# A four-layer graph kernel: products of the second pass during the neighbour search, norms on four row groups, and r and c of the last chunk from unscaled rows

## The chip, the cores and the metric

The kernel runs on one core of a Trainium2 chip. The metric is the time of one execution on the device in microseconds (us); lower is better. A core has TensorE (PE, matrix products; its weight loads are shown as PEld), VectorE (DVE), ScalarE (ACT), GpSimd (POOL), SyncE (SP, which here only issues transfers) and sixteen DMA engines. Each engine works through its own queue in order; between engines the program sets semaphores.

## The reference, cut to what matters

x is 2708 x 128, adj 2708 x 2708, both 32-bit floats. Four layers follow one another, each `x = layernorm(x + layer(x, adj))`. The change touches the first and the start of the second.

```python
def _L0_gnn_ref(x, A, W1, b1, W2, b2, sigma, k):       # sigma = 1, k = 4
    z = _lap_mul(A, x) @ W1 + b1                        # _lap_mul: d * (A @ (d * x)), d = 1/sqrt(row sums)
    z = leaky_relu(z, negative_slope=0.1)
    sq = sum(z * z, axis=-1)
    d2 = maximum(sq[:, None] + sq[None, :] - 2.0 * (z @ z.T), 0.0)
    S = exp(-sqrt(d2 + 1e-10) / (2.0 * sigma))
    S = where(ranks of -S in the row < k, S, 0.0)       # the k nearest of each node
    return _lap_mul(S + A, x) @ W2 + b2

def _L1_gnn_ref(X, A, W, a):
    XW = X @ W
    s_col, s_row = XW @ a[0, :f], XW @ a[0, f:]
    den = exp(leaky_relu(s_row[:, None] + s_col[None, :], negative_slope=0.01))
    num = A @ den
    att = where(num != 0, den / num, 0.0)
    return A @ (att @ XW)
```

The third layer is a normalised A times x times a matrix, the fourth a product of x and A @ x with a matrix, then a maximum with zero.

## The kernel before

**Tiles and chunks.** The 2708 nodes are 22 row tiles of 128 (`T`); the last, number 21 (`FULL`), has 20 rows (`LAST`). The columns are six chunks (`C`), four of 512 and one each of 384 (tiles 16 to 18) and 276 (tiles 19 to 21). Rows of the transposed adjacency for tiles 0 to 15 (`S` = 16) are streamed from memory in panels of four tiles by one chunk (`load_panel`, L171, issued by SP); those for tiles 16 to 21 stay in memory on the core (`res`).

**First pass and search (layer 0).** A first pass sums degrees and computes z, its transpose zT, and the negated square norms (`nsq`). `nsq3` holds the norms as three bf16 parts on three partitions; a product with ones (`ones3`) adds them to every row. The search runs over 22 tiles, in the order 4 to 15, 0 to 3, 16 to 21 (L623). For each, TensorE makes six norm products (L632) and six products of zT with itself (L642) into six accumulators, ACT copies these into a `key` tile (L643, three buffers), and VectorE finds the eight largest values of each row (MAX8, L644) and their places (FIND_INDEX8, L645). `z2`, the doubled rows, is made by ACT (L626).

**Weights.** `weigh` (L586) turns the distances of a batch of tiles into similarities (two operations on VectorE, a logarithm and two exponentials on ACT), degrees, and the scaled rows y2, writes these to `y2_rows` in memory, and calls `others` (L556), which separates the node itself from its neighbours. It runs in batches: tiles 0 to 16 after tile 16, 17 to 19 after tile 19, 20 and 21 at the end. A scheduler places the instructions of the search on each engine.

**Second pass.** `by_panels` (L189, products at L204) multiplies the adjacency with y2, chunk by chunk: 21 products a chunk, and one round for the 20 last rows for each group of three chunks (chunks share a call through the row groups, `few`). For chunk 0 the order is tiles 0 to 11, 16 to 19, 12 to 15, 20. Beside it runs a list of due work, `Due`: each product is a tick, and work is entered by its tick. `sum_near` (L678) adds, for each tile, three gathered rows of neighbours (L672, an indirect transfer by POOL, nine buffers) with weights on VectorE; it is due at ticks 24 + 23t/5. `end_pass2` (L825) enters, for each chunk: `finish` (add the neighbour sums with identity products, L692, and copy to `hT`, L832), `norm0` (product with W2, residual, layer norm), `turn` (transposes into `xT`), `find_c` (c, the column scores, on all rows, and its own entry `cc`), `times_w` and `keep_xw` (XW and its rows to memory), and for each tile `compare` (a 0/1 mask of c against the node's own c, L779; ties counted in L781), `rank_rows` (ACT sums the mask's rows, L792) and `rank_columns` (products with ones sum its columns into `rk`, L797). With both sums c of every node gets its rank. For the last tile `compare` sums its rows on VectorE itself (L774). The order on TensorE, VectorE and ACT is that of the program here.

**After the pass.** Ranks are put together (L918 to L923), `pick_c` (L927) picks c at some ranks, first "head", then "first", `to_all` and `on_all` spread values over the partitions by products, `gb` and `lc` are filled, and the sums of layer 1 by blocks of ranks run over the panels again (L1176), with further work put between them (`between`).

Of the kernel before, what the change touches and what calls it, by code (L numbers as in the profile page):

```python
# [8 lines left out]
F32 = mybir.dt.float32  # L9
# [21 lines left out]
class Due:  # L31


    def __init__(self):
        self.n, self.work = 0, []

    def at(self, n, f, *args):
        self.work.append((n, len(self.work), f, args))
        self.work.sort(key=lambda w: w[:2])
# [13 lines left out]
def kernel(  # L53
# [54 lines left out]
    mis_pool = psum.enter_context(tc.tile_pool(name="mis", bufs=2, space=bass.MemoryType.PSUM))  # L108
# [80 lines left out]
    def by_panels(weights, done, tick=None, ready=(), first=None):  # L189
# [6 lines left out]
        accs = {}  # L196

        def product(c, i, src, w):
            lhsT = weights(i)[few(c) if i == FULL else slice(None)]
            start = c not in accs  # L200
            if start:
                accs[c] = acc_tile()
            stop = tick is None and i == (FULL if c % GROUPS == 0 else FULL - 1)
            nc.tensor.matmul(accs[c][: lhsT.shape[-1], :w], lhsT=lhsT, rhs=src, start=start, stop=stop)  # L204

        for c in range(C):
            w = cw[c]
            for i in [*(first if first and c == 0 else range(FULL)), *([FULL] if c % GROUPS == 0 else [])]:
                if i == FULL:
                    for n in range(c, c + GROUPS):  # L210
                        product(n, i, res[few(n), i - S, cols[n]], cw[n])
                    done(c, accs[c])
                    for _ in range(GROUPS if tick is not None else 0):
                        tick()
                    continue
                if i < S:
                    if i % 4 == 0:
                        if ready:
                            part = ready.pop(0)
                        else:  # L220
                            part = load_panel(i // 4, c)
                    src = part[:, i % 4, :w]
                else:
                    src = res[:, i - S, cols[c]]
                product(c, i, src, w)
                if i == FULL - 1 and c % GROUPS:
                    done(c, accs[c])
                if tick is not None:
                    tick()

# [133 lines left out]
    with tc.tile_pool(name="knn", bufs=1) as knn:  # L364
        nsq = knn.tile([P, T], F32, tag="nsq", name="nsq")
        nsq3 = knn.tile([3, N], BF16, tag="nsq3", name="nsq3")
        ones3 = knn.tile([3, P], BF16, tag="ones3", name="ones3")
# [47 lines left out]
        def turn_norms(c, ts, parts):  # L415
# [4 lines left out]
            nc.scalar.copy(nsq3[:, cols[c]], ps[:3, : cw[c]])  # L420
# [1198 lines left out]
```

## Time and profile before

| what | us |
| --- | --- |
| median of seven runs | 1061.82 (1056.93 to 1068.3) |
| the profiled execution, time / span | 1063.85 / 1062.1 |
| PE busy / PEld busy in the span | 990.8 / 479.7 |
| DVE / ACT / POOL busy | 643.0 / 338.8 / 265.5 |
| search: first MAX8 starts, last FIND_INDEX8 ends | 167.61, 301.54 |
| second pass on PE: first product, end of the last identity products | 294.71, 421.70 |
| last copy to hT ends | 422.53 |
| "head" of the ranks starts | 439.27 |
| clock granted to TensorE, mean | 0.974 of full |

Times inside the span count from its start. A row of the groups names the line, the engine, the operation, its output and inputs with shapes, the count, then busy time, mean nanoseconds of one, and the engine's idle time just before such instructions with what ended most of it. A row of the timeline has start, duration, engine, line, operation, shapes and count, and in brackets the idle time ahead of it with its releaser. Products in 32-bit floats are two records each.

In the window 157 to 301.6, the search, PE is busy 143.38 us, DVE 136.41, ACT 78.36 and POOL 15.95 of 144.60.

### The profile page before, as it was taken

To read this page: it belongs to the slowest core of one execution; us is meant where nothing else is said; L and a number is where in the kernel's file an instruction comes from. 1 tells how busy PE (TensorE), PEld (TensorE's weight loads), DVE (VectorE), ACT (ScalarE), POOL (GpSimd) and SP (SyncE) were. 2 spreads that over 40 slices of the span, in tenths; PEclk is the share of its full clock that TensorE was granted. 3 is DMA by queue.
4 is the path that set the end of the run, shared out by engine and by line. 5 is a ranking of instruction groups with operands and counts; after the bars stand their busy time and mean duration, and the time that the engine had idled before them with its cause. 6 is when DMAs were issued, how large, how long until landed. Compare 5 with 4: busy or idle time off the path is not lost.

```text
span 1062.1 us, 11424 instructions
## 1 busy us (share of the span) xinstructions
PE 990.8 (93%) x3678; PEld 479.7 (45%) x3678; DVE 643.0 (61%) x1351; ACT 338.8 (32%) x614; POOL 265.5 (25%) x332
## 2 busy tenths in 40 slices
PE   0888999999999998699899999999999999999996
PEld 0346454444444556344333333334445544564444
DVE  5985438999965577763999999994111121222222
ACT  0000125555511246413767777662010100020000
POOL 4000000000457762117864444430121100000000
PEclk9989999999999999699999999999999999998998
DMA  9999350000068766399465545566565957574662
GB/s 339 365 343 250 113 174 1 0 1 0 11 217 262 224 179 216 136 350 277 129 180 132 143 136 168 137 173 219 197 218 145 316 170 228 144 261 147 225 174 67
DMA packets 109363, 190.30 MB, mean 179 GB/s; under 512 B 13650, under 2 KB 46690, under 8 KB 109294
## 3 DMA queue, kind: packets, MB, share of 16 engines
q1 hardware_dynamic: 91408, 151.79, 44.0%
q0 software_dynamic: 17712, 37.62, 12.8%
q8 instruction: 31, 0.51, 0.2%
q14 instruction: 38, 0.31, 0.1%
q10 hardware_dynamic: 174, 0.08, 0.0%
HBM read 214.37 MB, written 4.16 MB: 206 GB/s over the span
## 4 chain that ended last, share of the span: by engine, by line
PE 83%; DVE 5%; DMA 5%; POOL 3%; issue 2%; ACT 2%; SPq 0%; POOLq 0%; DVEq 0%; ACTq 0%
PE acc L204 36%; PE acc L642 9%; PE hacc L1280 9%; PE num L1423 8%; PE acc L428 8%; PE acc L632 2%; PE acc L1176 2%; DMA res<-in_adjT 2%; DMA ring<-in_adjT,slot_i 1%; PE mis L285 1%; DMA part<-in_adjT 1%; DVE mask L779 1%; DVE both L483 1%; POOL ring L125 1%; PE mis L1187 1%
## 5 line engine op out<-in xcount | busy, mean ns | idle before, releaser
L1301 POOL DMA_INDIRECT ring<-in_adjT,slot_i x88 | 98.3, 1116 | 100.6 <-PE num L1423 84.3
L1423 PE MATMUL num<-ring,lw 128*64 128x512 f32 (+1 forms) x528 | 113.7, 551 | 3.4 <-DVE err L1265 1.8
L1280 PE MATMUL hacc<-inv,xws 128*128 128x512 f32 (+1 forms) x264 | 111.7, 559 | 0.3 <-ACT inv L1258 0.3
L642 PE MATMUL acc<-zT,z 128*128 128x512 f32 (+4 forms) x264 | 108.3, 557 | 0.0
L1255 ACT ACTIVATE inv<-num,plain 128x1024 f32<-128x1024 f32 x88 | 80.5, 915 | 59.2 <-PE num L1423 56.5
L253 POOL TENSOR_TENSOR rstd<-rstd,minus_half 128x4 f32<-128x4 f32 (+1 forms) x19 | 18.2, 956 | 316.6 <-DVE rstd L252 316.6
L234 ACT COPY gb<-acc 128x512 f32<-128x512 f32 (+2 forms) x18 | 9.6, 534 | 252.7 <-PE acc L204 252.7
L643 ACT COPY key<-acc 128x512 f32<-128x512 f32 (+3 forms) x132 | 70.1, 534 | 59.8 <-issue 29.8
L204 PE MATMUL acc<-ring,y 128*128 128x512 f32 (+2 forms) x192 | 81.8, 555 | 0.5 <-POOL sim L579 0.5
L1265 DVE TENSOR_TENSOR err<-inv,num 128x1024 f32<-128x1024 f32 x88 | 74.4, 855 | 13.0 <-ACT inv L1258 12.3
L1280 PEld LDWEIGHTS hacc<-inv,xws 128*128 128x128 f32 x264 | 46.5, 189 | 77.2 <-issue 37.0
L204 PE MATMUL acc<-ring,xs 128*128 128x512 f32 (+2 forms) x192 | 78.2, 551 | 0.0
L1272 DVE SCALAR_TENSOR_TENSOR inv<-gb,g_inv,inv 128x1024 f32<-128x1024 f32 x88 | 77.1, 914 | 0.1
L672 POOL DMA_INDIRECT got<-y_rows,where x66 | 70.2, 1063 | 25.7 <-issue 8.2
L204 PE MATMUL acc<-ring,carry 128*128 128x512 f32 (+2 forms) x192 | 74.5, 542 | 0.0
L204 PE MATMUL acc<-ring,m_rows 128*128 128x512 f32 (+2 forms) x192 | 74.3, 542 | 0.0
L1269 DVE SCALAR_TENSOR_TENSOR inv<-err,inv 128x1024 f32<-128x1024 f32 x88 | 72.7, 865 | 0.1
L642 PEld LDWEIGHTS acc<-zT,z 128*128 128x128 f32 (+1 forms) x264 | 47.5, 188 | 55.0 <-issue 49.5
L570 POOL TENSOR_TENSOR slot_e<-near,sim 128x44 f32<-128x44 f32 (+2 forms) x3 | 0.7, 241 | 271.5 <-DVE d2inv L598 267.4
L1258 ACT ACTIVATE inv<-inv 128x1024 f32<-128x1024 f32 x88 | 67.6, 768 | 2.8
L644 DVE MAX8 near<-key 128x8 f32<-128x2708 f32 (+1 forms) x22 | 65.5, 2979 | 4.8 <-ACT key L643 4.8
L645 DVE FIND_INDEX8 where<-near,key 128x8 uint32<-128x2708 f32 (+1 forms) x22 | 65.4, 2972 | 0.0
(327 smaller groups left out, 1339.3 us busy)
## 6 DMA issues: line engine op xcount, KB each, us to landing
ring<-in_adjT SPq DMA_DIRECT2D x86, 1024.0 KB
ring<-in_adjT SPq DMA_DIRECT2D x19, 768.0 KB
part<-in_adjT SPq DMA_DIRECT2D x12, 1024.0 KB
ring<-in_adjT SPq DMA_DIRECT2D x19, 552.0 KB
res<-in_adjT SPq DMA_DIRECT2D x4, 1280.0 KB
more<-in_adjT SPq DMA_DIRECT2D x4, 1024.0 KB
part<-in_adjT SPq DMA_DIRECT2D x3, 768.0 KB
part<-in_adjT SPq DMA_DIRECT2D x3, 552.0 KB
```

The source lines that it names most:

```text
L204: nc.tensor.matmul(accs[c][: lhsT.shape[-1], :w], lhsT=lhsT, rhs=src, start=start, stop=stop)
L428: nc.tensor.matmul(accs[c][:, : cw[c]], lhsT=y[:, i, :], rhs=src[:, : cw[c]], start=first, stop=last)
L642: nc.tensor.matmul(pks[c][:p, : cw[c]], lhsT=z2[:, :p], rhs=zT[:, cs], start=False, stop=True)
L643: nc.scalar.copy(key[:p, cs], pks[c][:p, : cw[c]])
L672: nc.gpsimd.indirect_dma_start(out=got[:p, :], out_offset=None, in_=y2_rows[:, :], in_offset=bass.IndirectOffsetOnAxis(ap=where[:p, t, k : ...
L1255: nc.scalar.activation(inv, num[:, :w], AF.Ln, scale=plain[:, 0:1], bias=plain[:, 1:2])
L1265: nc.vector.tensor_mul(err, inv, num[:, :w])
L1269: nc.vector.scalar_tensor_tensor(inv, err, 2.0, inv, op0=ALU.subtract, op1=ALU.mult)
L1272: nc.vector.scalar_tensor_tensor(inv, gb[:, col : col + w], g_inv[:, q : q + 1], inv, op0=ALU.max, op1=ALU.mult)
L1280: nc.tensor.matmul(haccs[:, o:e], lhsT=xws[:, q, :], rhs=inv[:, o:e], start=(q == 0), stop=(q == NQ - 1))
L1301: nc.gpsimd.indirect_dma_start(out=rows[i][:KC, n, :], out_offset=None, in_=adj_half[:, :], in_offset=bass.IndirectOffsetOnAxis(ap=slot_i[ ...
L1423: nc.tensor.matmul(num[n * (BJ + 2) : (n + 1) * (BJ + 2), o:e], lhsT=lw[:, 2 * q + n, :], rhs=rows[i][:, n, c0 + o : c0 + e], start=True, ...
```

## The change

- The norm products lie on four row groups: the norm rows and the ones are held at partitions 0, 32, 64 and 96, copied there by three transfers on SP's queue ahead of the panels. Tile 4, the first of the search, still uses the first group alone.
- Twelve products of chunk 0 of the second pass (tiles 4 to 15) are issued during the search, one in each of the tiles 6 to 17 of its order, into an accumulator of their own. The panels of chunk 0 are loaded in the order 1, 2, 3, 0, and a panel of chunk 1 when one is used up. On TensorE the order is that of the program from the second tile.
- `weigh` runs in six calls: tiles 4 to 7, 8 to 11, 12 to 15 and 0 to 3 with their adds on POOL, 16 to 19 and 20 to 21 with their adds on VectorE.
- The second pass takes chunk 0's products of tiles 0 to 3 and 16 to 19, four of chunk 1, then the rest; the due ticks are moved.
- For the last chunk (tiles 19 to 21) the rows are turned before they are normalised; r and c come from products of the raw rows with two columns of weights, corrected with mean and standard deviation. `last_norm` and `last_xw` normalise the rows and make XW later, in the sums of layer 1.
- The mask of tile 20 is made in two halves, the second summed on VectorE. The comparison of tile 21 with all columns is replaced by one of all nodes with its 20 columns (`compare_few`). Rank constants (`fold`, `sel`, `rk_f`) move to the start of the second pass, into the memory of `near`.

The diff, cut to its core:

```diff
-        nsq3 = knn.tile([3, N], BF16, tag="nsq3", name="nsq3")
-        ones3 = knn.tile([3, P], BF16, tag="ones3", name="ones3")
+        NORMS = 4
+        nsq3 = knn.tile([32 * NORMS, N], BF16, tag="nsq3", name="nsq3")
+        ones3 = knn.tile([32 * NORMS, P], BF16, tag="ones3", name="ones3")
...
+        w_rc = wae[:, D:]
+        w_sum = atile([2], "w_sum")
+        ps = mis_tile()
+        nc.tensor.matmul(ps[:, :2], lhsT=ones_f, rhs=w_rc, start=True, stop=True)
+        nc.vector.tensor_copy(w_sum, ps[:, :2])
...
-        def weigh(ts):
+        def weigh(ts, engine):
...
-            nc.vector.tensor_add(nr, nr, nsq[:, t0:t1, None].to_broadcast([P, t1 - t0, TOPK]))
-            nc.vector.tensor_scalar(nr, nr, 0.0, DIST_EPS, op0=ALU.min, op1=ALU.subtract)
+            engine.tensor_add(nr, nr, nsq[:, t0:t1, None].to_broadcast([P, t1 - t0, TOPK]))
+            engine.tensor_scalar(nr, nr, 0.0, DIST_EPS, op0=ALU.min, op1=ALU.subtract)
...
-            nc.vector.tensor_reduce(dd, sm, AX.X, ALU.add)
-            nc.vector.tensor_add(dd, dd, deg[:, t0:t1])
+            if engine is nc.vector:
+                nc.vector.tensor_reduce(dd, sm, AX.X, ALU.add)
+                nc.vector.tensor_add(dd, dd, deg[:, t0:t1])
+            else:
+                engine.tensor_add(dd, sm[:, :, 0], deg[:, t0:t1])
+                for k in range(1, TOPK):
+                    engine.tensor_add(dd, dd, sm[:, :, k])
...
-        ready = [load_panel(g, 0) for g in range(G)]
+        mis_psum.close()
+        first_psum = ExitStack()
+        first_pool = first_psum.enter_context(
+            tc.tile_pool(name="first", bufs=1, space=bass.MemoryType.PSUM, side="right")
+        )
+        acc0 = first_pool.tile([P, CW], F32, tag="first", name="acc0")
+        for g in range(1, NORMS):
+            nc.sync.dma_start(nsq3[32 * g : 32 * g + 3, :], nsq3[:3, :])
+        AHEAD = range(4, S)
+        panels0 = {g: load_panel(g, 0) for g in (*range(1, G), 0)}
+        ready = [panels0[0]]
+        batches = {7: range(4, 8), 11: range(8, 12), 15: range(12, 16), 3: range(4), T - 3: range(S, T - 2)}
...
+                if n == 1:
+                    search.enter_context(tc.manual_schedule(engines={nc.tensor.engine}))
...
-                    cs = cols[c]
-                    nc.tensor.matmul(pks[c][:p, : cw[c]], lhsT=ones3[:, :p], rhs=nsq3[:, cs], start=True, stop=False)
+                    r = slice(32 * (c % NORMS), 32 * (c % NORMS) + 3) if n else slice(3)
+                    nc.tensor.matmul(
+                        pks[c][:p, : cw[c]], lhsT=ones3[r, :p], rhs=nsq3[r, cols[c]], start=True, stop=False
+                    )
...
+                i = n - 2
+                if i in AHEAD:
+                    nc.tensor.matmul(
+                        acc0[:, : cw[0]], lhsT=y2[:, i, :], rhs=panels0[i // 4][:, i % 4, : cw[0]],
+                        start=(i == AHEAD[0]), stop=False,
+                    )
+                    if i % 4 == 3:
+                        ready.append(load_panel(len(ready) - 1, 1))
...
-                if t == T - 6:
-                    weigh(range(0, T - 5))
-                if t == T - 3:
-                    weigh(range(T - 5, T - 2))
-            weigh(range(T - 2, T))
+                if t in batches:
+                    weigh(batches[t], nc.gpsimd if t < T - 3 else nc.vector)
+            weigh(range(T - 2, T), nc.vector)
...
+    spare = near.rearrange("p t k -> p (t k)")
+    few_n, rk_f, neg_r = (spare[:, n * T : (n + 1) * T] for n in range(3))
+    fold, sel = spare[:, 3 * T : 3 * T + 2 * NCH], spare[:, 3 * T + 2 * NCH : 3 * T + 2 * NCH + 2 * NB]
+    nc.vector.memset(rk_f, float(OOB))
+    nc.vector.tensor_add(fold, ident[:, : 2 * NCH], ident[:, 32 : 32 + 2 * NCH])
...
-    def norm0(ts, power=False):
+    def norm0(ts, raw=False):
...
-        normalize(ts, xs, power)
+        if not raw:
+            normalize(ts, xs)
...
+    def rc_of(c, p_of):
+        ts = chunk_tiles[c]
+        po = mis_tile()
+        for k, t in enumerate(ts):
+            p, o = p_of(t), t * P - starts[c]
+            nc.tensor.matmul(po[:p, 2 * k : 2 * k + 2], lhsT=xTs[c][:, o : o + p], rhs=w_rc, start=True, stop=True)
+        return po[:, : 2 * len(ts)].rearrange("p (k v) -> p v k", v=2)
...
+    def last_rc():
+
+        both = rc_of(C - 1, lambda t: P)
+        for v, dst in ((1, cc), (0, rr)):
+            nc.vector.scalar_tensor_tensor(
+                dst[:, l0:l1], mv[:, l0:l1, 0], w_sum[:, v : v + 1], both[:, v, :], op0=ALU.mult, op1=ALU.subtract
+            )
+            nc.vector.scalar_tensor_tensor(
+                dst[:, l0:l1], dst[:, l0:l1], -1.0, rstd_l, op0=ALU.mult, op1=ALU.mult
+            )
+
+    def last_norm():
+        for t in last_ts:
+            nc.vector.tensor_scalar(
+                xs[: pw[t], t, :], xs[: pw[t], t, :], mv[: pw[t], t, 0:1], rstd_l[: pw[t], t - l0 : t - l0 + 1],
+                op0=ALU.subtract, op1=ALU.mult,
+            )
+
+    def turn_c(c):
+
+        pc = mis_tile()
+        for t in chunk_tiles[c]:
             o = t * P - starts[c]
...
+            nc.tensor.transpose(pc[:, o : o + P], cc[:, t : t + 1].to_broadcast([P, P]), ident)
+        nc.scalar.copy(c_row[:, cols[c]], pc[:, : cw[c]])
...
+    split = {T - 2: (T - 1) * P // 2}
...
+        m = split.get(t, o + p)
+        nc.vector.tensor_scalar(mask[:p, :m], c_row[:p, :m], s, None, op0=ALU.is_ge)
+        if m < o + p:
             nc.vector.tensor_scalar(
...
+                mask[:p, m : o + p], c_row[:p, m : o + p], s, 0.0, op0=ALU.is_ge, op1=ALU.add, accum_out=rows_h[:p],
+            )
...
+    def compare_few():
+
+        grid = [P, T, LAST]
...
+        nc.vector.tensor_tensor(
+            few_m, cc[:, :, None].to_broadcast(grid), c_row[:, None, FULL * P :].to_broadcast(grid), op=ALU.is_ge
+        )
+        for u in range(T):
+            nc.tensor.matmul(
+                rk[:LAST, T - 1 : T], lhsT=few_m[: pw[u], u, :], rhs=ones_b[: pw[u], :1], start=False,
+                stop=(u == T - 1), skip_group_check=True,
+            )
+        nc.vector.tensor_reduce(few_n, few_m, AX.X, ALU.add)
+        own_ties(T - 1)
...
-    near_at = [24 + (23 * t) // 5 for t in range(T)]
+    near_at = [23 + (21 * t) // 5 for t in range(T)]
...
-                    at(n + 17 + 2 * k, rank_columns, t)
+                    at(n + (20 if c < C - 2 else 18) + 2 * k, rank_columns, t)
...
-            at(n + 1, exp_table)
             at(n + 2, norm0, ts, True)
-            at(n + 3, turn, c)
-            at(n + 4, find_c, c)
-            for t in ts:
-                at(n + 4, times_w, c, t)
-            at(n + 4, keep_xw, c)
...
+            at(n + 2, turn, c, True)
+            at(n + 2, exp_table)
+            at(n + 2, find_r)
+            at(n + 3, last_stats)
+            at(n + 3, last_rc)
+            at(n + 3, turn_c, c)
+            at(n + 3, negate_r)
+            for k, t in enumerate(ts[:-1]):
+                at(n + 4 + k, compare, t)
+                at(n + 4 + k, rank_rows, t)
+                at(n + 5 + k, rank_columns, t)
+            at(n + 3 + len(ts), compare_few)
+            at(n + 4 + len(ts), exp_r)
...
-        by_panels(
-            rows_of(y2), end_pass2, due.tick, ready, [*range(S - 4), *range(S, T - 2), *range(S - 4, S), T - 2]
-        )
+        tail = [FULL - 1, FULL]
+        order = [*((0, i) for i in (*range(4), *range(S, FULL - 1))), *((1, i) for i in range(4))]
+        order += [*((0, i) for i in tail), *((1, i) for i in range(4, FULL))]
+        order += [(c, i) for c in range(2, C) for i in [*range(FULL), *([FULL] if c % GROUPS == 0 else [])]]
+        by_panels(rows_of(y2), end_pass2, due.tick, ready, order, {0: acc0})
...
         c_part = pick_c(edge, "first")
+        last_norm()
+
+        def last_xw():
+
+            for t in last_ts:
+                p = pw[t]
+                pt = mis_tile()
+                nc.tensor.transpose(pt[:, :p], xs[:p, t, :], ident[:p, :p])
+                xT = small.tile([P, P], F32, tag="z", name="xT")
+                nc.scalar.copy(xT[:, :p], pt[:, :p])
+                po = mis_tile()
+                nc.tensor.matmul(po[:p, :D], lhsT=xT[:, :p], rhs=wa_sb, start=True, stop=True)
+                row = small.tile([P, P], F32, tag="junk", name="row")
+                nc.scalar.copy(row[:p], po[:p, :D])
+                nc.gpsimd.dma_start(xw_rows[t * P : t * P + p, :], row[:p])
...
+            if (c, i0) == (0, 4):
+                last_xw()
```

## The prediction

> **What bounds the kernel now.** I read the page's table of costliest groups, then one tile of the search, then busy time by stage, the chain of waits, and the end of the second pass instruction by instruction. First the groups; a row ends with busy time, mean ns of one, and the idle time ahead of it with its releaser.
>
> ```profile
> L642 PE MATMUL acc<-zT,z 128*128 128x512 f32 (+4 forms) x264 | 108.3, 557 | 0.0
> ...
> L644 DVE MAX8 near<-key 128x8 f32<-128x2708 f32 (+1 forms) x22 | 65.5, 2979 | 4.8 <-ACT key L643 4.8
> L645 DVE FIND_INDEX8 where<-near,key 128x8 uint32<-128x2708 f32 (+1 forms) x22 | 65.4, 2972 | 0.0
> ```
>
> The search has two full engines. VectorE needs 2.98 + 2.97 = 5.95 us a tile, and its whole idle time, 4.8 us, lies in the first two tiles. One tile in the timeline (start, duration):
>
> ```profile
> 270.29 1.31 PE L632 MATMUL acc<-nsq,ones 3*128 3x512 bf16 x6
> 270.81 2.98 DVE L644 MAX8 near<-key 128x8 f32<-128x2708 f32 x1
> 271.53 4.81 PE L642 MATMUL acc<-zT,z 128*128 128x512 f32 x12
> ```
>
> The next norms start at 276.27, so TensorE's period is 5.98 us too. Shortening norms alone gives VectorE nothing. Then the hand-over to the second pass:
>
> ```profile
> 292.53 2.97 DVE L645 FIND_INDEX8 where<-near,key 128x8 uint32<-128x2708 f32 x1
> 294.71 10.54 PE L204 MATMUL acc<-ring,y 128*128 128x512 f32 x24 [0.51 <-POOL sim L579]
> 298.58 2.96 DVE L645 FIND_INDEX8 where<-near,key 20x8 uint32<-20x2708 f32 x1
> 301.67 0.20 ACT L599 ACTIVATE d2inv<-d2inv 128x3 f32<-128x3 f32 x1 [5.37 <-DVE d2inv L598]
> 302.19 0.83 POOL L602 TENSOR_TENSOR y<-xs,d2inv 128x384 f32<-128x384 f32 x1
> ```
>
> TensorE starts the pass at 294.71, before the last find ends at 301.54: rows of tiles 0 to 16 are ready. Those of 17 to 19 are ready at 303.02, 1.5 us behind the last find, with no wait, since ten products are still ahead of them. Busy time by stage:
>
> ```profile
> 294.70:330.00 35.30, 35.28 (x92) 15.85 (x93) 18.03 (x48) 3.82 (x16) 21.05 (x37) 1.00 0.75 247
> 390.00:410.00 20.00, 17.91 (x132) 12.53 (x130) 17.82 (x65) 7.82 (x15) 12.79 (x12) 1.00 0.64 185
> 410.00:424.00 14.00, 13.20 (x115) 10.50 (x115) 8.61 (x28) 10.86 (x16) 1.60 (x2) 0.88 0.76 251
> 424.00:454.00 30.00, 18.51 (x155) 11.00 (x159) 24.44 (x74) 12.59 (x25) 3.87 (x3) 0.72 0.46 165
> ```
>
> (Columns: length, then PE, weight loads, DVE, ACT, POOL; the granted clock.) The pass is TensorE's until 390; then VectorE is nearly full too; 424 to 454 is a chain of small steps at a low clock. The chain's large pieces there:
>
> ```profile
> 428.75 1.30 PE mis L744 x2
> 431.09 1.46 DVE mask L779
> 432.82 1.53 DVE mask L779
> 434.72 2.96 DVE mask L774 x2
> ```
>
> **The change, part by part.**
>
> *Norms on four row groups.* Before: six in 1.25 us. The nearest row of short contractions on separate groups is L443, 12 records over three groups in 1.98 us, against 4.74 for the same columns on full rows (L642). By that ratio, 2.4, norms take 0.5; bounds 0.45 and 1.25. I take 0.5: a TensorE period of 5.3, which VectorE hides; the worth is the room it makes. "TensorEngine Tiling (Array Packing)", Key Properties, speaks against: a change of tiling mode drains the engine, twice a tile here. No run here shows the drain alone; L443's row contains it once. If a drain ate the gain, norms would stay at 1.25.
>
> *Twelve products during tiles 6 to 17.* 12 x 0.88 = 10.5 us leave the second pass (24 records took 10.54). TensorE's period there is 0.5 + 4.74 + 0.87 = 6.1, which the new waits below cover; with norms at 1.25 it is 6.85, 0.87 over VectorE's, twelve times, less some 8 us of those waits: +2.5.
>
> *Rows weighed in five batches.* The products need y2 early, so the weighing is cut up, and four batches put their adds on POOL. The order of the built program shows where that bites. POOL's first add (L598 of the changed kernel) waits for the batch's last find; ACT's logarithm (L600) waits for POOL, and in ACT's queue it stands ahead of the last key copy of tiles 8, 12 and 16, for which the next max waits. Per batch: two POOL steps at 0.30 spacing (L578 to L579 at 293.25 and 293.55), a logarithm 0.24 (L593 to L594), the copy 0.39, some 0.15 between engines: 1.4 us in which VectorE stands. Three times: 4.2. At the first batch the logarithm stands behind tile 4's copies and delays tile 5's: 0.4. Four comparisons (L574) between max and find: 4 x 0.15 = 0.6. The moved fold (L750, L752) reuses near's memory and waits, behind tile 8's find, for POOL's last use of it: POOL's four sums 1.0, ACT 0.5, row scaling 1.1 (4/3 of 0.83), DMA issue 1.2 (L610, mean 1.23) and ten steps of 0.25 end about 1 us after that find; with its own 0.55: 1.6. The memset L749 behind tile 16's find waits likewise: 1.1. Sum 7.9, less 0.9 for the small operations which stood among before's finds (126.5 us for 21 periods of 5.98). Bounds: 0, if POOL and ACT are always in time, to 10.
>
> *Start.* Tile 1's norms wait for three copies of the norm rows on SP's queue, ahead of the panels. Nearest row: the row write issued at 304.75 frees the gather at 308.87. So 2 to 4 us from the cast's end (165.48) instead of norms at 166.89, less about 0.9 of faster norms: -0.3 to +1.7, taken 0.5. VectorE is waiting there (L644's idle), so it counts. The panels have 100 us of cover.
>
> The last find ends at 301.5 + 7.9 - 0.9 + 0.5 = 309.0.
>
> *Second pass.* Order now: four products with tiles 0 to 3, then 16 to 19. The batch 16 to 19 closes 1.9 us behind the last find (before's 1.5, with four tiles scaled for three and a larger reduce). TensorE ends the search 7.3 us ahead of the last find as before, does four products, and stands from about 305 to 310.9. 16 products are done then, so the pass ends 310.9 + (421.7 - 294.7) - 16 x 0.86 = 424.1 instead of 421.7. Generally, end moves by (last find - 306.6): **gain only if the search grows by less than 5.1 us**. It grows by 7.5: +2.4. After the wait TensorE may run slowly: at 168.4 the twelve records of tile 1 took 6.20 instead of 4.74 at a clock of 0.79. I take those 1.4; bounds 0 to 1.7. "TensorE: Matmul & The Clock Gate", Part 1, states half clock after about 3.4 us of idling until as much busy time; that would be 1.7 and the sum 0.3 more.
>
> *End of the pass.* Ticks go from 132 to 120 and near sums from every 4.6 to every 4.2; chunk 4's masks then come later against the end. VectorE was at 17.82 of 20 from 390 to 410, and ACT has two mask sums, 2.25 and 2.12, ahead of the last xT copy. 0 to +1.5, taken 0.5. Gathers: 66 at 1.30 from 7.3 us behind the last find end at 413, two us ahead of the last near sum's tick.
>
> *Tail.* Before, the head starts 439.27 - 422.53 = 16.7 us after the last hT copy. After: transposes without the statistics; xT copy behind both mask sums, 4.9; r and c 1.5; transposes of c and copy 1.1; masks 1.54 + 0.33 + 0.85 + 1.55 + 0.37 = 4.6; the 20 columns (440 elements compared, reduced, ties) 1.45; seven small rank operations 1.4: 14.9. Gain 1.8, and 0.2 for fold and sel, whose six operations mostly lay in the wait for c_head. But last_norm, three scalings (0.85, L277), now stands behind the first picking on VectorE, which TensorE waits for at 453 (2.28 idle): +0.85. last_xw's nine TensorE steps and three row writes go into that idle time; uncovered, 1.5 to 3. Tail -1.2, bounds -3.2 to +1.
>
> **Sum** on the profiled execution, 1063.85 (span 1062.1): 2.4 + 1.4 + 0.5 - 1.2 = +3.1, 1067.0. That execution lies 2.0 above the median of the runs, 1061.82; on the median it is **1065**.
>
> **Rivals.**
>
> *The search doesn't grow* (POOL and ACT in time: batches are small, 128x16). For it: POOL is idle through the search (16 busy of 145 us). Against: the wait is in order, not load. Last find 301.5: -5.1, tail -1.2, no cold start: 1055.5; with the tail at its best 1053, with half of the stalls 1059.
>
> *VectorE or POOL takes over the end of the pass, and norms don't overlap.* The later find moves gathers to end at 413 to 416; if they pass the near sums' ticks, each us counts whole, from a last find at about 311. With +2.5 for norms the find is there. For it: VectorE's 17.82 of 20. Price 2.5 + 1.0 for start + 1.0 + up to 3: 1068 to 1074.
>
> *The products do not leave the path*: the gate at tiles 16 to 19 takes back all but six of sixteen. This is in the forecast already; with a find at 306.6, the pass gains nothing and the tail's -1.2 stays: 1060.6.
>
> **How the numbers follow.** Forecast (1060.6 to 1069, with the last rival) 0.45; search unchanged 0.33; end taken over 0.22. What can be told from no change is 0.5%, 5.3 us: 1056.5 to 1067.1. Faster: 0.26 from the second case. Within: 0.33 of the forecast, 0.07 and 0.02: 0.42. Slower: 0.12 + 0.20. The range, 1053 to 1073, leaves out the far end of the third case and little of the second; the forecast's own is 1060 to 1069.
>
> **What would show it.** VectorE idle before MAX8 of tiles 8, 12, 16, released by ACT's copies, 1.4 each; a wait at the fold released by POOL; the last find near 309; norms at 0.5 for six; TensorE idle about 6 us ahead of the product with tile 16, released by POOL; head 15 us after the last hT copy. Wrong if finds follow each other without gaps, or if TensorE stays the search's bound.

## The result and the profile after

| | before | changed |
| --- | --- | --- |
| median, us | 1062.80 (64 runs, 1056.93 to 1069.82) | 1069.77 (27 runs, 1065.48 to 1073.20) |
| ratio, 95% interval | 1 | 1.0063 (1.0050 to 1.0077) |
| profiled execution, time / span | 1063.85 / 1062.1 | 1071.51 / 1069.8 |
| granted clock, mean | 0.974 | 0.968 |

The changed kernel is slower by 0.63%, some 7 us: inside the range given, 0.8 above the forecast's own 1060.6 to 1069, on the side that the sum (+3.1) pointed to, and more than twice as far.

Profiles of one kernel differ in when the search begins: the first MAX8 started between 165.8 and 170.0 in the profiles of this study, on the same code too. So places in the program are counted here from the start of the first MAX8. "Pass end" is the end of the last identity products, "block stage" the first products with the block layer's weights (`num`).

| us from the first MAX8 | before | changed | difference |
| --- | --- | --- | --- |
| second MAX8 starts | 7.43 | 10.28 | +2.85 |
| last FIND_INDEX8 ends | 133.93 | 145.59 | +11.66 |
| pass end | 254.09 | 261.85 | +7.76 |
| head of the ranks starts | 271.66 | 280.26 | +8.60 |
| block stage starts | 333.77 | 342.39 | +8.62 |

All of the loss is there by the ranks. The block layer keeps its pace (223.7 before, 223.6 after); what follows was 3.1 shorter in this one execution, on untouched code, and it was 333.4 to 337.4 over all profiles, so that is chance.

The same groups of the page as shown of before (columns as there):

```profile
L669 PE MATMUL acc<-zT,z 128*128 128x512 f32 (+4 forms) x264 | 113.0, 577 | 0.0
...
L679 DVE MAX8 near<-key 128x8 f32<-128x2708 f32 (+1 forms) x22 | 65.4, 2972 | 13.6 <-ACT key L670 12.2
...
L680 DVE FIND_INDEX8 where<-near,key 128x8 uint32<-128x2708 f32 (+1 forms) x22 | 65.4, 2972 | 0.0
```

MAX8 and FIND_INDEX8 cost what they did. VectorE's idle time before MAX8 grew from 4.8 to 13.6, and ScalarE's key copies (L670) ended 12.2 of it. One such gap, in the timelines of VectorE, POOL and ScalarE of the changed kernel:

```profile
273.92 2.97 DVE L680 FIND_INDEX8 where<-near,key 128x8 uint32<-128x2708 f32 x1
276.98 0.21 POOL L598 TENSOR_TENSOR near<-near,nsq 128x16 f32<-128x16 f32 x1 [17.82 <-DVE where L680]
277.27 0.27 POOL L599 TENSOR_SCALAR near<-near 128x16 f32<-128x16 f32 x1
277.58 0.22 ACT L600 ACTIVATE sim<-near 128x16 f32<-128x16 f32 x1 [1.08 <-POOL near L599]
277.70 0.37 ACT L670 COPY key<-acc 128x276 f32<-128x276 f32 x1
278.10 2.98 DVE L679 MAX8 near<-key 128x8 f32<-128x2708 f32 x1 [1.21 <-ACT key L670]
```

This is the predicted chain, link by link: the find ends at 276.89, POOL adds, ScalarE takes the logarithm, and only then makes the last 276 columns of a key whose products had long ended. ScalarE stood idle 1.08 us with that copy ready behind the waiting logarithm. It happens at tiles 8, 12 and 16 of the order (1.20, 1.21, 1.21). The two predicted waits for the memory of `near`:

```profile
231.76 0.18 DVE L750 TENSOR_TENSOR near<-ident 128x22 f32<-128x22 f32 x1 [1.39 <-POOL slot_e L585]
...
285.56 2.96 DVE L679 MAX8 near<-key 128x8 f32<-128x2708 f32 x1 [1.39 <-issue]
285.56 0.08 DVE L749 MEMSET near<- 128x22 f32 x1
```

The memset (L749) stands ahead of the MAX8 in the queue; the timeline gives the gap of both to the MAX8 and names no releaser. Then TensorE at the start of the search, and at its end:

```profile
170.29 0.37 PE L657 MATMUL acc<-nsq,ones 3*128 3x512 bf16 x1 [0.67 <-DMA nsq<-nsq]
171.03 1.25 PE L657 MATMUL acc<-nsq,ones 3*128 3x512 bf16 x4 [0.37 <-DMA nsq<-nsq]
172.21 7.57 PE L669 MATMUL acc<-zT,z 128*128 128x512 f32 x12
...
201.67 2.39 PE L657 MATMUL acc<-nsq,ones 3*128 3x512 bf16 x6
203.99 6.51 PE L669 MATMUL acc<-zT,z 128*128 128x512 f32 x12
...
265.08 0.55 PE L657 MATMUL acc<-nsq,ones 3*128 3x512 bf16 x6
265.56 4.81 PE L669 MATMUL acc<-zT,z 128*128 128x512 f32 x12
270.21 1.02 PE L673 MATMUL acc<-ring,y 128*128 128x512 f32 x2
...
305.52 3.70 PE L206 MATMUL acc<-ring,y 128*128 128x512 f32 x8
317.30 2.93 PE L206 MATMUL acc<-res,y 128*128 128x512 f32 x3 [8.08 <-POOL y L614]
```

The norms do overlap: six in 0.55 beside a chunk product (0.82 elsewhere), in place of 1.25. But twelve product records that take 4.81 took 7.57 behind the wait for the copies and 6.51 behind ScalarE's first batch: TensorE had been waiting and ran slow (granted clock 0.64 from 204 to 208). At the end it stands 8.08 us for the rows of tile 16, 1.75 behind the last find (315.55). This wait for the last batch's rows is called the gate below. Behind tile 12's logarithm TensorE stands too, and the twelve records after it are as slow:

```profile
251.50 0.27 PE L657 MATMUL acc<-nsq,ones 3*128 3x276 bf16 x1 [2.60 <-ACT key L670]
251.71 6.51 PE L669 MATMUL acc<-zT,z 128*128 128x512 f32 x12
```

The busy time by stage (columns as before):

```profile
301.60:315.00 13.40, 7.62 (x19) 2.34 (x17) 13.40 (x11) 3.82 (x10) 2.10 (x13) 0.97 0.24 78
315.00:330.00 15.00, 12.70 (x28) 5.30 (x29) 7.80 (x30) 2.00 (x10) 7.97 (x12) 0.79 0.28 82
```

### The profile page after: what moved, and what is told of

Same layout as the page of the kernel before. It is cut to its first block, busy times and chain, and to the rows that moved or that the text cites. A ratio compares the mean times of both kernels' runs of the same rounds, so it can differ in the third digit from the quotient of the medians.

```text
span 1069.8 us, 11538 instructions
## 1 busy us (share of the span) xinstructions
PE 987.6 (92%) x3691; PEld 476.0 (44%) x3691; DVE 642.3 (60%) x1352; ACT 340.0 (32%) x634; POOL 278.1 (26%) x392
## 4 chain that ended last, share of the span: by engine, by line
PE 71%; DVE 16%; DMA 5%; ACT 3%; issue 2%; POOL 2%; SPq 1%; POOLq 0%; DVEq 0%; ACTq 0%
PE acc L206 34%; PE num L1550 9%; PE hacc L1407 9%; PE acc L430 7%; DVE where L680 5%; DVE near L679 5%; DMA res<-in_adjT 3%; PE acc L1301 3%; PE acc L669 2%; DVE mask L868 1%; PE mis L286 1%; ACT junk L886 1%; DMA part<-in_adjT 1%; DVE both L485 1%; POOL ring L127 1%
## 5 line engine op out<-in xcount | busy, mean ns | idle before, releaser
L669 PE MATMUL acc<-zT,z 128*128 128x512 f32 (+4 forms) x264 | 113.0, 577 | 0.0
L670 ACT COPY key<-acc 128x512 f32<-128x512 f32 (+3 forms) x132 | 69.6, 534 | 55.4 <-PE acc L669 46.2
L1392 DVE TENSOR_TENSOR err<-inv,num 128x1024 f32<-128x1024 f32 x88 | 74.4, 855 | 13.0 <-ACT inv L1385 12.2
L679 DVE MAX8 near<-key 128x8 f32<-128x2708 f32 (+1 forms) x22 | 65.4, 2972 | 13.6 <-ACT key L670 12.2
L206 PE MATMUL acc<-ring,y 128*128 128x512 f32 (+2 forms) x168 | 68.8, 539 | 0.0
L1550 PEld LDWEIGHTS num<-ring,lw 128*64 128x64 f32 x528 | 36.2, 136 | 62.4 <-issue 41.7
```

Source lines behind the costliest of these rows:

```text
L669: nc.tensor.matmul(pks[c][:p, : cw[c]], lhsT=z2[:, :p], rhs=zT[:, cs], start=False, stop=True)
L679: nc.vector.max(near[:p, t, :], key[:p])
L1392: nc.vector.tensor_mul(err, inv, num[:, :w])
L1550: nc.tensor.matmul(num[n * (BJ + 2) : (n + 1) * (BJ + 2), o:e], lhsT=lw[:, 2 * q + n, :], rhs=rows[i][:, n, c0 + o : c0 + e], start=True, ...
```

## The experiments

Ratios are to the kernel before on the same chip, 95% interval in brackets. All changes of places are from the first MAX8, one profile each. The stretch from the first to the second MAX8 differs by itself: with the same code in the search it was 7.49 in the run of the three edits and 9.14 and 5.98 in two later ones.

**Constants out of the search.**

```diff
-    nc.vector.memset(rk_f, float(OOB))
-    nc.vector.tensor_add(fold, ident[:, : 2 * NCH], ident[:, 32 : 32 + 2 * NCH])
+    def fill_spare():
+        nc.vector.memset(rk_f, float(OOB))
+        nc.vector.tensor_add(fold, ident[:, : 2 * NCH], ident[:, 32 : 32 + 2 * NCH])
...
+    at(near_at[0] + 1, fill_spare)
```

> The changed kernel with one edit: the constants that lie in near's memory (fold, sel, the memset of rk_f) are made one tick behind the first near sum, where VectorE is half idle, so they no longer stand between two finds. Measured from the start of the first MAX8 to the end of the last FIND_INDEX8 the search took 133.9 us before and 145.5 in the changed kernel. Theory (each in-order wait on VectorE adds to the search, and the search sets the end): the waits of 1.39 behind tile 8's find and 1.39 behind tile 16's and 0.55 of work go, the search takes 142.2, TensorE's wait for tile 16's rows ends 3.3 earlier and the time falls by about 3. Rival (TensorE's 6.1 us a tile is the real bound of these tiles and VectorE merely waits elsewhere): the next MAX8 waits for its key instead, the search stays at 145, the time within 1 us.

Measured: 1066.84, ratio 1.0026 (1.0006 to 1.0046), 2.9 below the changed kernel; last find at 140.80, 4.8 earlier. The two waits are gone and nothing took their place; with them went tile 13's gap of 1.12, which was not among those named. For the search the theory holds. Of the 4.8, only 2.3 are left at the pass end: from the gate on, the same TensorE records took 117.0 in place of 114.5, with the same idle time but a lower granted clock (0.86 for 0.90 in the first 20 us, 0.89 for 1.00 in the last 15).

**ScalarE's logarithms a tile later.**

```diff
-                    search.enter_context(tc.manual_schedule(engines={nc.tensor.engine}))
+                    search.enter_context(tc.manual_schedule(engines={nc.tensor.engine, nc.scalar.engine}))
...
-                if t in batches:
-                    weigh(batches[t], nc.gpsimd if t < T - 3 else nc.vector)
+                if n + 1 < T:
+                    z2_next = times_two(walk[n + 1])
+                for step in rest:
+                    next(step, None)
+                rest = []
+                if n and walk[n - 1] in batches:
+                    b = walk[n - 1]
+                    rest = [weigh(batches[b], nc.gpsimd if b < T - 3 else nc.vector)]
+                    next(rest[0])
```

`weigh` yields once, behind the third activation.

> The changed kernel with ScalarE in program order during the search and the weighing of a batch put one tile later on it: logarithm and exponentials behind all key copies of the tile after the batch's last one, the rest one tile further; the doubled rows of the next tile stand ahead of them. Theory (ScalarE's logarithm ahead of the last key copy makes MAX8 of tiles 8, 12, 16 late, and by a starved and then slow TensorE those of 6 and 13): 1.20 + 1.21 + 1.21 + 0.79 + 1.12 = 5.5 us go, the search takes 140.0 instead of 145.5, the time falls by about 5. Rival (ScalarE merely waits somewhere else in order, and the twelve products wait for the later rows): stalls of the same sum appear at tiles 5, 9, 13, 17, search 144 to 147, time within 1.5 us.

Measured: 1059.68, ratio 0.9964 (0.9942 to 0.9986): 10 below the changed kernel and below the kernel before. The last find is at 140.28, near the expected 140.0, in part by luck. The five gaps named (5.5) are gone, and of the two waits for the memory of `near` 0.28 and 0.31 are left; but at the last tile two new waits came, 0.78 and this one:

```profile
302.07 2.97 DVE L685 MAX8 near<-key 20x8 f32<-20x2708 f32 x1 [2.18 <-ACT key L676]
```

There the logarithm of tiles 16 to 19 stands ahead of all six key copies: the same fault, and all the later runs with this edit keep it. Twice the expected time came. TensorE's row says why:

```profile
303.55 2.93 PE L206 MATMUL acc<-res,y 128*128 128x512 f32 x3 [5.48 <-POOL y L615]
```

The last find ended at 308.11 here. In program order the batch of tiles 16 to 19 was weighed before it, so the gate opened 4.6 us ahead of the last find in place of 1.75 behind: this edit moved two things, the search by 5.3 and the gate by 6.3 more.

**The second tile's norms without copies.**

```diff
-                    r = slice(32 * (c % NORMS), 32 * (c % NORMS) + 3) if n else slice(3)
+                    r = slice(32 * (c % NORMS), 32 * (c % NORMS) + 3) if n > 1 else slice(3)
```

> The changed kernel, but the second tile of the search too takes all its norms from the first row group, so it needs none of the three copies of the norm rows. In the changed kernel its first MAX8 lies 10.28 us behind the one before it, in the kernel before 7.43. Theory (the copies' landing, 1.0 us of waits, and the clock that falls while TensorE waits, 7.57 us for twelve records in place of 6.20, make 2.9 us): 7.5 to 8.0 us, the search 143, the time 2 to 2.5 lower. Rival (the clock is low there in any case and only the 1.0 of waits goes): 9.2 us, search 144.4, time 1 lower.

Measured: the second MAX8 at 7.43 as before the change, the last find at 142.64, as the theory has it, but 1070.27, ratio 1.0058 (1.0034 to 1.0082): no gain in time. In its profile the pass end is only 0.16 earlier: from the gate on, the same 499 TensorE records take 117.3 in place of 114.5, with the same idle time (3.7) but a lower granted clock (0.85 for 0.90 in the first 20 us, 0.89 for 1.00 in the last 15). The head is 1.35 earlier, and the sums of layer 1 take 2.7 longer than in the changed kernel's. Why the clock and these sums differ isn't shown. The cost of the copies to the search is shown, its worth in time is not.

**The tail alone.** The search, norms, batches, order of products and ticks are those of before; the tail is the changed one, with the constants late.

```diff
-        batches = {7: range(4, 8), 11: range(8, 12), 15: range(12, 16), 3: range(4), T - 3: range(S, T - 2)}
+        batches = {T - 6: range(0, T - 5), T - 3: range(T - 5, T - 2)}
...
-    near_at = [23 + (21 * t) // 5 for t in range(T)]
+    near_at = [24 + (23 * t) // 5 for t in range(T)]
```

> The tail of the change alone: last chunk's r and c from raw rows, masks of tile 20 in halves, the comparison with 20 columns, later XW, with the search, the norms, the batches, the order of products and the ticks of the kernel before. Prediction's step: from the last copy to hT to the head 14.9 us instead of 16.7, less 0.85 behind it, the time 1.2 below the kernel before (bounds 3.2 below to 1 above). In the changed kernel that stretch took 16.3, with two mask sums of ScalarE ahead of the last xT copy. Rival (the loss of the change lies in the tail): 3 or more above the kernel before. If the masks are late only because of the later search, this run shows xT's copy 4.5 or less behind hT's and a stretch near 15.

Measured: 1058.30, ratio 0.9943 (0.9920 to 0.9966), 5 below the kernel before. ScalarE at the last hT copy, in the changed kernel and then in this one:

```profile
431.36 2.02 ACT L886 ACTIVATE junk<-mask 128x2176 bf16<-128x2176 bf16 x1 [0.71 <-DVE mask L868]
433.52 0.39 ACT L956 COPY hT<-acc 128x276 f32<-128x276 f32 x1
434.63 2.23 ACT L886 ACTIVATE junk<-mask 128x2432 bf16<-128x2432 bf16 x1 [0.72 <-DVE mask L868]
436.99 2.12 ACT L886 ACTIVATE junk<-mask 128x2304 bf16<-128x2304 bf16 x1
439.26 0.48 ACT L785 COPY xT<-mis 128x384 f32<-128x384 f32 x1
```

```profile
417.20 2.02 ACT L868 ACTIVATE junk<-mask 128x2176 bf16<-128x2176 bf16 x1 [0.71 <-DVE mask L850]
419.36 2.12 ACT L868 ACTIVATE junk<-mask 128x2304 bf16<-128x2304 bf16 x1
421.62 0.40 ACT L939 COPY hT<-acc 128x276 f32<-128x276 f32 x1
421.90 2.25 ACT L868 ACTIVATE junk<-mask 128x2432 bf16<-128x2432 bf16 x1
424.57 0.48 ACT L767 COPY xT<-mis 128x384 f32<-128x384 f32 x1 [0.33 <-PE mis L764]
```

With chunk 4 finished in time, one mask sum lies between the copies and xT comes 2.55 behind hT's copy, not 5.35. The head follows the hT copy by 13.2, against 16.3 in the changed kernel and 16.7 before. So the tail is the good part of the change, and the changed kernel hid it. At the block stage 2.3 of the gain are left (331.43 against 333.77); where the rest of the 5 in the medians arises isn't shown.

**The gate alone.** Order of the second pass, the search untouched.

```diff
-        order = [*((0, i) for i in (*range(4), *range(S, FULL - 1))), *((1, i) for i in range(4))]
-        order += [*((0, i) for i in tail), *((1, i) for i in range(4, FULL))]
+        order = [*((0, i) for i in range(4)), *((1, i) for i in range(S))]
+        order += [*((0, i) for i in range(S, FULL + 1)), *((1, i) for i in range(S, FULL))]
```

> The changed kernel with another order of the second pass alone: chunk 0 with tiles 0 to 3, then chunk 1 with tiles 0 to 15 (whose rows are ready), then chunk 0 with tiles 16 to 21 and chunk 1 with 16 to 20. The search is left as it is. Theory (behind the search TensorE stands 8.1 us for the rows of tiles 16 to 19 and then runs 2 to 3 us slow): twelve more products fill the wait, TensorE doesn't stand between search and pass, the pass ends about 9 us earlier counted from the first MAX8, and the time falls by 8 to 10, to about 1061. Rival (the gathers, which start 7 us behind the last find, or the near sums on VectorE hold the end whatever TensorE does): TensorE's wait only moves to chunk 1's or 2's identity products, the end of the pass stays within 3 us, the time falls by 3 or less.

Measured: 1067.34, ratio 1.0062 (1.0038 to 1.0086), no gain on the changed kernel's ratio of 1.0063; the pass end 2.75 earlier. TensorE's longest wait between search and tail:

```profile
PE acc L724 <- DVE near_sum L717: 5.0, 1, 5.0
```

(total, times, longest.) The rival holds: the wait for tile 16 went, and 5.0 of it came back as a wait for near sums. These wait for gathered rows in their turn (VectorE stands 8.0 and 3.8 for them), and POOL issues the gathers 1.3 apart. Behind a late find the pass is held twice.

**Repairs together.** First the three edits of constants, logarithms and second tile's norms.

> The three edits of the first round together: constants of near's memory late, ScalarE's logarithms a tile later, norms of the second tile from the first row group. In the logarithm run the time had fallen by 10 against 5 expected, because the batch of tiles 16 to 19 was weighed 7 us ahead there as well (its wait ended 4.6 us before the last find instead of 1.8 behind). Theory (waits add up on one path): search 140.3 less 0.3 and 2.9, about 137 from the first MAX8; TensorE's wait ends about 133 behind it; time 1056. Rival (beyond the gate something else sets the end, so the earlier search is lost): time within 1.5 of the logarithm run's 1059.7.

Measured: 1055.08, ratio 0.9944 (0.9923 to 0.9966); last find at 136.32; TensorE's wait (4.2) ends 131.8 behind the first MAX8; pass end 247.41, 14.4 before the changed kernel's. The waits add up as the theory says.

Then with the other order of the second pass:

> The three edits and the other order of the second pass. Theory: the 5 us wait for tiles 16 to 19 and the slow clock behind it go too; TensorE passes from search to second pass without a wait over 1 us; time 1056 less 5 to 7, about 1050. Rival (gathers and near sums set the end now: 66 gathers at 1.30 from 7 us behind the last find, then near sums): 1054 to 1056, with TensorE waiting for near sums at the chunks' ends.

Measured: 1056.17, ratio 0.9954 (0.9931 to 0.9977). The gate's wait is gone, but the pass end lies 115.7 behind the last find, against 111.1 in the three edits' run. There is no gain, as the rival had it, but not for its reason: TensorE waits only 0.4 for near sums. It waits 2.7 for the last tile's key copies, behind the logarithm, and 3.2 for rows of a layer norm late in the pass, and from the end of the search to the pass end the same 510 records are busy 119.1 in place of 115.6, at a granted clock of 0.95 for 0.97. With earlier ticks on top:

```diff
-    near_at = [23 + (21 * t) // 5 for t in range(T)]
+    near_at = [20 + 4 * t for t in range(T)]
```

> The former with near sums due at ticks 20 + 4t in place of 23 + 21t/5, so that chunk 4 is finished at tick 99 in place of 105 of 120 and its three masks and ScalarE's mask sums come ahead of the last chunk. In the tail-alone run xT's copy came 2.6 us behind the last hT copy and the head 13.2 behind it; in the changed kernel 5.4 and 16.3, with two mask sums of ScalarE between. Theory (the compressed end of the pass took the tail's gain back): xT at 2.6 to 3.5, head at 13.2 to 14.5, time 2 to 4 below the former run. Rival (near sums then wait for gathers at 1.30 each, 3.9 us a tile against 4 ticks of 0.93): TensorE waits at the chunks' ends and the time is the same or higher.

Measured: 1054.16, ratio 0.9938 (0.9914 to 0.9962). xT comes 2.4 and the head 12.8 behind the hT copy, so the tail has its gain back; the pass end is as late behind the last find as in the former. The time is 2 lower, within the intervals.

**Ticks alone, and four products ahead.** The three edits with these ticks and the order of the changed kernel; then with chunk 1's four ready products put ahead of tiles 16 to 19.

> The three edits (constants late, logarithms a tile later, second tile's norms from one group) with near sums due at 20 + 4t, the order of products as in the changed kernel. Theory (the mask sums that fall behind the last hT copy hold the tail): xT 2.6 to 3.5 behind hT's copy, head at 13.2 to 14 behind it instead of 16.3, pass end as in the three edits' run (111 behind the last find), time about 3 below its 1055. Rival (near sums that are due earlier wait for gathers, and TensorE for them): pass end 114 or more behind the last find, time 1054 to 1056.

> The former with chunk 1's four ready products put ahead of tiles 16 to 19 of chunk 0. Theory (TensorE's wait of 4.2 for those rows lies on the path): 3.5 us of the wait are filled, the pass ends 3 us earlier, time 2 to 3 below the former. Rival (the near sums, which follow the last find by the gathers' pace, hold the end already): pass end unchanged within 1 us, counted from the last find, and time the same.

Measured: 1057.90, ratio 0.9949 (0.9924 to 0.9974), and 1055.96, ratio 0.9935 (0.9911 to 0.9958). With the ticks alone xT comes 2.4 and the head 12.8 behind the hT copy, but the pass end 118.9 behind the last find: the rival holds. What the tail gains the pass gives back, and more: the head is at 268.38, against 265.83 in the three edits' run. With the four products the pass end is 115.6 behind, 3.2 earlier, as the theory has it, but the wait wasn't filled. TensorE stands 4.2 as before, in two pieces, 2.74 for the last tile's key copies and 1.48 for the rows, and in the 28 us from the end of the search products the granted clock is 1.00 in place of 0.88. Why the clock stays isn't shown. The head is at 263.66, the earliest of all, 8.0 earlier than in the kernel before; 1.5 of that is chance, from a second MAX8 5.98 behind the first (7.49 in the run with the ticks alone). This kernel and the one with the ticks and the other order (0.9938) have the lowest ratios, 0.6% below the kernel before and 1.3% below the changed one, but their intervals cover those of the three edits and of the tail alone.

**One row group in the repaired kernel.** All norms from the first group.

> The former with all norm products on the first row group, so that six take 1.25 us again in place of 0.55 to 0.82. Theory (with VectorE no longer waiting elsewhere, TensorE's 1.25 + 4.74 + 0.87 = 6.86 a tile in tiles 6 to 17 is over VectorE's 5.98): up to 0.88 a tile, the search 5 to 10 us longer and the time 5 to 8 more, so the row groups are what makes the twelve products fit. Rival (slack at key buffers covers it): search within 2 us, time within 2.

Measured: 1065.54, ratio 1.0041 (1.0016 to 1.0066), 9.6 above the former; the last find 10.5 later, both a little more than expected. VectorE now waits before each MAX8 of tiles 7 to 18, for instance:

```profile
264.00 2.98 DVE L685 MAX8 near<-key 128x8 f32<-128x2708 f32 x1 [0.78 <-ACT key L676]
270.84 2.98 DVE L685 MAX8 near<-key 128x8 f32<-128x2708 f32 x1 [0.77 <-ACT key L676]
```

The period is 6.84; 1.25, 4.74 and 0.87 make 6.86. The twelve products fit only with the row groups.

**The tail alone again**, beside these three.

> The tail alone with the search of the kernel before, once more, on the chip of the other three, to say what the products during a mended search are worth beside it. Theory (the tail's gain of about 3.5 in the head and the search's of about 3 add up): this run lies 3 to 6 above the run with the ticks. Rival (the search's products are worth nothing even when mended): the two are within 1.5.

Measured: 1057.15, ratio 0.9947 (0.9924 to 0.9970), 1.2 above the run with four products and 0.8 below the one with the ticks alone, and the intervals cover each other. The rival holds: what the mended search adds to the tail in time can't be told from nothing, although in the profiles with the four products the block stage starts 5.5 earlier than with the tail alone (325.80 against 331.31; 4.0 when both are counted from the second MAX8).

## Why the prediction was right, and where not

**The search grows by in-order waits: right, too small.** Predicted from the first MAX8: 7.0 of waits, net, and 0.5 at the start. Measured: 8.8 and 2.85. The three gaps behind ScalarE's logarithm (1.2 each for 1.4), the fold (1.39 and 0.55 for 1.6) and the memset (1.39 for 1.1) are near what was worked out. For the first batch 0.4 was put down at tile 5; 0.79 came, at tile 6. The gap of 1.12 at tile 13 was missed. At both, a wait of ScalarE also starves TensorE, which then runs the next tile slowly (6.51 for 4.81). The start, 2.85, is outside the bounds given (-0.3 to +1.7): the copies cost 1.0 of waiting, but the slow clock behind them made the twelve records 1.4 longer than before's slow ones (7.57 for 6.20), and the prediction's 0.9 for faster norms did not come: the four behind the wait took 1.25.

**The gate and the formula: right.** The gate was set at 1.9 behind the last find and is at 1.75. TensorE stood 8.08 there, not about 6: it ended the search's products 10.0 ahead of the last find, not 7.3. From there the pass took 114.5 (114.6 by the working, 113.2 and 1.4 for the clock). That it agrees to 0.1 is partly luck: the clock took 2.0 there, not 1.4. Since the find was late by more than 5.1, the sixteen early products gave a loss; with the gate ahead of the find they gave a gain at the pass end, 3.1 with the logarithms later and 6.7 with the three edits. The rule was good, its assumption of a gate tied to the last find was one of this order alone.

**The end of the pass and the tail: mis-sized.** The prediction took +0.5 for the compressed end and -1.2 for the tail. Together they came to +0.86 at the block stage: the last hT copy ends 1.27 later behind the pass end than before (0.5 was taken), xT comes 5.34 behind it (4.9), and the steps from there to the head take 10.97 (10.0). Alone, the tail is worth 3.4 at the head and 5 in time. The step that failed is "xT copy behind both mask sums, 4.9", which was put down to the tail itself: both sums lie there only because chunk 4 is finished at tick 105 of 120, as the runs with the earlier ticks show (2.4). The mask sums cost nearly 3 us at xT's copy, and another delays the hT copy by 1.3.

**Two sums that don't come out.** Sixty-six gathers at 1.30 from 7.3 behind a find at 309.0 end at 402, not 413; 413 goes with the 97 us that the 66 took before. They took 98 in the changed kernel, from 8.0 behind the find, and TensorE didn't wait for near sums. The last rival's terms on 1065 end at 1072.5, not 1074.

**The norms: right in kind.** 0.55 to 0.82 for 0.5, and one row group costs 9.6 us. The Trainium skill ("TensorEngine Tiling (Array Packing)", Key Properties) says that a change of tiling mode drains the engine. No drain shows up in these rows that would eat the gain.

**The clock after a wait.** The records behind ScalarE's first batch took 6.51 for 4.81, 1.7 more, and so did those behind tile 12's logarithm. Behind the 8 us at the gate the profile's granted clock over 20 us was 0.90, so 2.0 at full speed were lost there, for 1.4 taken; in the run with the second tile's norms it was 0.85 behind the same wait, so 3.0 were lost. The Trainium skill ("TensorE: Matmul & The Clock Gate", Part 1) has about 3.4 us at half clock after an idle stretch as long, which gives an estimate of 1.7. The first price agrees, but not its condition: from 200 to 204 TensorE stood idle for 0.33 in all, and behind tile 12 it stood 2.60. The loss at the gate is larger than the rule's.

**The rivals.** "The search doesn't grow" fell. "VectorE takes over the end of the pass" was not the changed kernel's cause: TensorE doesn't wait for near sums there. It stands close behind: in the gate run TensorE waited 5.0 for near sums, and they for POOL's gathers; in the runs with the other order or the earlier ticks it waited 0.4 to 2.6. Sum: predicted +3.1; by the profile +8.6 at the block stage; by medians +7.0. Of the 5.5 between the first two, 4.0 are there at the pass end (7.76 for 3.8), from a search 4.2 longer than predicted, and 1.5 come between the pass end and the block stage (+0.86 for -0.7).

## What to carry to other kernels

Work that is hidden under a full engine must not put a waiting instruction ahead of that engine's supply: a 0.2 us logarithm that waits for POOL, standing before a 0.4 us copy, cost 1.2 us each time, and memory that is used again brought waits of the same kind; look at the order of every queue, not at busy shares. Moving such an instruction one tile later helped at every tile but the last, where it then stood ahead of six copies and cost 3.0. When work is taken out of a stage, ask what opens the stage behind it: here the last batch's rows, not TensorE's work, set the start, and once that was open in the gate run, a wait for gathered rows took 5.0 of it back. Measure the parts of a compound change alone: one part here was worth 5 us and the whole lost 7.

## What the runs showed of the hardware that was not expected

- Six norm products on four row groups took 0.55 us in tiles with a chunk product ahead of them and 0.82 in the others. What makes the difference isn't shown.
- In four kernels with the same code ahead of it, the first MAX8 started anywhere from 165.8 to 170.0, and over all profiles the stretch from the end of the block layer, the same in all, took 333.4 to 337.4. Parts worth under 4 us can be read only from places in the trace, not from one span.
- Places differ by themselves too: behind the gate the same 499 records with the same idle time took 114.5 to 117.3, with the granted clock.
